# Layer 1 of a two-layer convolution and recurrence kernel: half of each normalized column copied across the partitions by GpSimd instead of by DMA transfers

## The chip, the cores and the metric

The kernel runs on one core of a Trainium2 chip. Its time is the device time of one execution in microseconds (us). The core has five engines that matter here: TensorE for matrix products (in the profile PE, with PEld for the loading of its weights), VectorE (DVE), ScalarE (ACT), GpSimd (POOL) and SyncE (SP), which in this kernel only issues transfers. Each engine has its own stream of instructions and works through it in order. Transfers (DMA) run beside the engines, on 16 DMA engines that all queues share. An engine waits for another, or for a transfer, by a semaphore.

## The reference

An image batch x of shape 4 x 64 x 256 x 256 (images, channels, rows, columns) goes through two layers, each x + f(groupnorm(x)). Layer 0 is a 1x1 and a 3x3 convolution, a product of spectra over 8x8 patches, a norm over channels and a gate. Layer 1, which the change touches, is a recurrence over the columns of the image:

```python
x = x + _L0_conv_ref(_gn(x), ...)
x = x + _L1_conv_ref(_gn(x), ...)
# inside _L1_conv_ref, f[w] is column w of the normalized image, (images, rows, channels)
def step(prev_col, cur_col):
    nb = jnp.concatenate([pad, prev_col, pad], axis=1)
    x = jnp.concatenate([nb[:, :-2], nb[:, 1:-1], nb[:, 2:]], axis=-1)
    new = _gru_cell(x, cur_col, w_ih, w_hh, b_ih, b_hh)   # shapes left out
    return (new, new)
_, outs = jax.lax.scan(step, f[0], f[1:])
```

The cell takes three rows of the previous column's result as input (192 channels in, "taps") and the current column as its hidden value ("own", 64 channels in). It has three gates: r and z by a sigmoid, n by a tanh, and new = (1 - z) n + z h. Column w can't be finished before column w - 1 is: 255 steps, each over 4 images x 256 rows x 64 channels.

## The kernel before

Layer 0 works in 32 blocks and takes about the first 4299 us; the change leaves it as it is. Between the layers stand a few small operations for the second group norm.

Layer 1 keeps a column of the four images as a tile of 128 partitions by 2 slots by 256 rows. A partition half holds the 64 channels of one image, so that four images fill two halves times two slots. Which image lies where changes from column to column: SLOTS lists slot by slot the images of the two halves, ((0, 1), (2, 3)) for even columns and ((0, 2), (1, 3)) for odd ones. The reason is the matrix unit. One matmul here uses a quarter of it, 64 rows by 64 columns, and quarters() issues four that can run side by side, one for each pair (r, c) of an input half r and an output half c. The taps read the previous state at half r, slot c and write the result at half c, slot r. So a column comes out with halves and slots exchanged, and the odd and even layouts follow from that.

The own part of a column must land in the same place, at half c, slot r. For r = c the normalized column xn has it in the right half. For r and c different, the image lies in the wrong partition half: its input must first be brought to the other half. That is what the tile xt is for: it holds, for each of 8 columns of a block, the two images that must cross over, slot 0 of the second half in the first half, and slot 1 of the first half in the second half. In column(), own() reads xn for r == c and xt otherwise.

The stages of a column and who does them:

- load_columns(w) issues, on SP's queue, three transfers for two columns of raw values, 16 columns ahead of their use. raws has three buffers of 8 columns (WB = 8).
- normalize(w, slot) is one ScalarE activation per slot. It is called for column w + 8 inside state(w, part), after the r gate's sigmoid of that part: slot 0 in part 0, slot 1 in part 1. So the normalized columns, and xt, run 8 columns ahead of their use. xns and xts have two buffers of 8 columns.
- In normalize, after slot 1 of every odd column, two transfers on SP's queue fill xt for two columns.
- column(w) issues the matmuls. A column is worked in two parts of its rows. parts(w) sets the cut, which moves up by one row per column and jumps back every 32 columns (SKEW), so that a part needs only rows of the previous column that are already done; part 0 has from 144 down to 113 rows. For each part: own and taps of r, for part 0 also own of n for the whole column, then taps of n, own and taps of z.
- state(w, part) turns the sums into the new state: sigmoid r (ACT), n = (hn + b) r + in (two VectorE operations that read the sums), sigmoid z and tanh (ACT), then g = (z - 1) h, n z, and st = n z - g on VectorE.
- add(w), on GpSimd, adds the state to the raw column, 128 x 512; after each odd column three transfers on SP's queue write the pair of columns out.
- empty_states(n) zeroes, on GpSimd, the edge rows of the next block of states, once every 8 columns.

The program order of the engines is the order in which the code issues. Ahead of the loop stand the loads of 16 columns, the normalizing of columns 0 to 8 with their xt, and empty_states(0). In the loop over w come empty_states for the next block (every 8 columns), column(w) with its two states (and in them normalize of column w + 8), add(w), and after odd columns load_columns. On SP's queue a pair of columns is therefore two xt transfers, three of out, three of raw, each waiting in its turn; on GpSimd's there is one add per column and two memsets per 8 columns.

All of the kernel's instructions pass through a helper that keeps the program order (line 158), so the profile names line 158 for nearly all of them; rows are told apart by their tiles: pshr, pshn, psni, pshz are the sums of the gates, st the state, wh and wi the weights of own and taps.

Of the kernel before, what the change touches and what calls it, by code (L numbers as in the profile page):

```python
# [16 lines left out]
B, C, W, H = 4, 64, 256, 256  # L17
# [146 lines left out]
def tile_conv_then_gru(  # L164
# [18 lines left out]
    nc = InOrder(tc, tc.nc)  # L183
# [109 lines left out]
    with layer0 as s:  # L293
# [20 lines left out]
        def normalize(n, jq):  # L314

            t, b, at = xq[n, jq], n // 8, n % 8
            flat = t.rearrange("p j k -> p (j k)")
            shift, rstd = sc0[:, b, 0:1], sc0[:, b, 1:2]
            if jq == 3:
                nc.vector.tensor_scalar(flat, flat, rstd, shift, ALU.mult, ALU.add)  # L320
            else:
                nc.scalar.activation(flat, flat, AF.Identity, bias=shift, scale=rstd)
            grid = t.rearrange("p j (r c) -> p j r c", c=10)
            if jq % 2 == 0:
                nc.gpsimd.memset(grid[:, 0, :, 0:1], 0.0)
            else:
                nc.gpsimd.memset(grid[:, 15, :, 9:10], 0.0)
            if at == 0 and jq < 2:
                nc.gpsimd.memset(grid[0:C, :, 0, :], 0.0)
            if at == 7 and jq >= 2:  # L330
                nc.gpsimd.memset(grid[C:P, :, 9, :], 0.0)
# [297 lines left out]
        for jq in range(4):  # L629
            normalize(0, jq)  # L630
        norm = None
        for n in range(NBLK + 1):
# [60 lines left out]
            for k in range(8):  # L693
                if k in (0, 3, 6):
                    pv = psum(4)
                    values(n, k, pv[:, 0:2])
                elif k in (1, 4, 7):
                    values(n, k, pv[:, 2:4])
                    keep_values(k - 1, 2, pv)
                else:  # L700
                    pv = psum()
                    values(n, k, pv)
                    keep_values(k, 1, pv)
                if k in (0, 2):
                    next(norm)
                if k in (1, 2, 4) and n + 1 < NBLK:
                    normalize(n + 1, k // 2)
                if k in (3, 4, 6):
                    next(norm)
                if k == 5 and n + 1 < NBLK:  # L710
                    normalize(n + 1, 3)
# [24 lines left out]
    with ExitStack() as s:  # L736
# [4 lines left out]
        raws, xns, xts, stcols = {}, {}, {}, {}  # L741
# [15 lines left out]
        def new_columns(n):  # L757
            xns[n] = colp.tile([P, 2, WB, H], F32, tag="xn", name=f"xn_{n}")
            xts[n] = colp.tile([P, WB, H], F32, tag="xt", name=f"xt_{n}")
# [6 lines left out]
        def normalize(w, slot):  # L766
            n, i = w // WB, w % WB
            if i == slot == 0:
                new_columns(n)
            nc.scalar.activation(  # L770
                xns[n][:, slot, i],
                raws[n][:, slot, i],
                AF.Identity,
                bias=sc1[:, w % 2, slot, 0:1],
                scale=sc1[:, w % 2, slot, 1:2],
            )
            if slot and i % 2:

                for half in range(2):
                    nc.sync.dma_start(  # L780
                        xts[n][half * C : (half + 1) * C, i - 1 : i + 1],
                        xns[n][(1 - half) * C : (2 - half) * C, half, i - 1 : i + 1],
                    )

        def add(w):
# [96 lines left out]
        for w in range(W):  # L882
            n, i = w // WB, w % WB
# [68 lines left out]
```

## Time and profile before

| | us |
|---|---|
| median of 3 runs | 5828.33 |
| lowest and highest run | 5819.98, 5828.91 |
| the profiled execution's own time | 5838.45 |
| its span, first to last instruction | 5836.7 |

The profile shows one execution. Busy time is the time in which an engine worked on an instruction; it does not tell whether anybody waited for it. Times on the timelines are counted from the start of the span. In a row, "out<-in" are the program's tiles, the shape is partitions x elements, "x" a count; in brackets stands how long the engine had been idle before, and what ended that. "issue" as the releaser means that nothing the profile shows had been waited for. A row of a queue (SPq) is the issuing of a transfer, not the transfer itself.

GpSimd's share of layer 1 before (from 4300 us on, columns: operation, tiles, shape and count, then busy us, mean ns of one, and idle time before with its releasers):

```profile
L158 POOL TENSOR_TENSOR raw<-raw,st 128x512 f32<-128x512 f32 x256 | 303.4, 1185 | 1151.4 <-ACT xn L158 569.2 <-DVE st L158 353.4 <-DMA raw<-x 156.6
L158 POOL MEMSET st<- 128x16 f32 x60 | 5.1, 128 | 71.2 <-PE pshz L158 71.2
```

Of the page's list of transfers these belong to layer 1 (count and size of each):

```profile
raw<-x SPq DMA_DIRECT2D x128, 256.0 KB
raw<-x SPq DMA_DIRECT2D x256, 128.0 KB
xt<-xn SPq DMA_DIRECT2D x256, 128.0 KB
out<-raw SPq DMA_DIRECT2D x128, 256.0 KB
```

The list is cut there at its end; the smaller transfers of out are not on the page.

### The profile page before, as it was taken

How to read it: one execution, taken by the hardware profiler on the slowest of the kernel's cores; microseconds unless marked ns; L12 is line 12 of the kernel's file. 1: busy time of each engine (PE TensorE's matmuls, PEld its weight loads, DVE VectorE, ACT ScalarE, POOL GpSimd, SP SyncE). 2: the span in 40 equal slices, each digit the busy share in tenths (PEclk: the TensorE clock that was granted, in tenths of full speed). 3: DMA queues.
4: the chain of work that ended last, by engine and by line, in shares of the span. 5: the costliest groups of instructions: out<-in, count | busy, mean ns of one | idle time of the engine just before them, and what ended most of it. 6: DMA issues, size and time to landing. Idle time of an engine off the chain costs nothing. (4 is left out here: it accounts for less than half of the span.)

```text
span 5836.7 us, 278467 instructions
## 1 busy us (share of the span) xinstructions
PE 5472.7 (94%) x127204; PEld 4752.8 (81%) x127204; DVE 4076.5 (70%) x9593; ACT 3475.0 (60%) x4604; POOL 476.3 (8%) x749
## 2 busy tenths in 40 slices
PE   4999999999999999999999999999979999999998
PEld 3888888778878888888878888888768888888888
DVE  4777677777777777766777677666667776777766
ACT  3656666556566666556556666565556665666655
POOL 0000000000000000000000000000002221222212
PEclk9999999999999999999999999999989999999999
DMA  7555555555555555555555554544444444444443
GB/s 251 149 153 157 154 155 142 149 158 150 152 150 156 154 146 141 160 149 148 151 144 152 143 134 130 145 133 129 136 116 115 117 114 112 115 117 116 119 112 84
DMA packets 557274, 818.28 MB, mean 140 GB/s; under 512 B 37484, under 2 KB 431632, under 8 KB 553712
## 3 DMA queue, kind: packets, MB, share of 16 engines
q1 hardware_dynamic: 522256, 634.46, 40.4%
q0 software_dynamic: 33552, 165.43, 8.9%
q8 instruction: 996, 16.32, 1.2%
q14 instruction: 182, 1.49, 0.1%
q10 hardware_dynamic: 288, 0.58, 0.0%
HBM read 622.72 MB, written 144.05 MB: 131 GB/s over the span
## 5 line engine op out<-in xcount | busy, mean ns | idle before, releaser
L158 PEld LDWEIGHTS psring<-h,t 100*32 100x32 f32 x40960 | 1333.4, 115 | 303.9 <-issue 200.6
L158 PE MATMUL psring<-h,t 100*32 100x128 f32 x40960 | 1445.3, 274 | 115.3 <-issue 41.4
L158 PEld LDWEIGHTS psring<-w_sb,xq 64*100 64x100 f32 x24576 | 1355.8, 163 | 81.4 <-issue 51.1
L158 PE MATMUL psring<-w_sb,xq 64*100 64x128 f32 x24576 | 1399.9, 271 | 21.6 <-issue 7.6
L158 ACT COPY h<-psring 100x1024 f32<-100x1024 f32 x1274 | 1205.7, 1026 | 162.8 <-PE psring L158 154.4
L158 DVE TENSOR_TENSOR pr<-psring,q 128x512 f32<-128x512 f32 (+1 forms) x576 | 462.9, 857 | 336.5 <-PE psring L158 326.4
L158 DVE BATCH_NORM_STATS2 lnst<-z 128x6 f32<-128x64 f32 x4096 | 545.7, 216 | 117.6 <-ACT z L158 117.6
L158 DVE TENSOR_TENSOR z<-z,lnm 128x1024 f32<-128x1024 f32 x512 | 612.8, 1218 | 8.7
L158 ACT COPY q<-psring 128x1024 f32<-128x1024 f32 x256 | 259.3, 1013 | 527.4 <-PE psring L158 445.3
L158 ACT ACTIVATE z<-pshz,b_rz 128x288 f32<-128x288 f32 (+7 forms) x510 | 242.5, 476 | 520.6 <-PE pshz L158 520.6
L158 PE MATMUL pshr<-st,wi 64*64 64x144 f32 (+7 forms) x12240 | 511.2, 270 | 42.0 <-issue 26.1
L158 ACT COPY z<-psring 128x2048 f32<-128x2048 f32 x128 | 238.9, 1867 | 520.9 <-PE psring L158 520.9
L158 PE MATMUL pshz<-st,wi 64*64 64x144 f32 (+7 forms) x12240 | 513.0, 271 | 25.3 <-issue 24.0
L158 PE MATMUL psni<-st,wi 64*64 64x144 f32 (+7 forms) x12240 | 510.2, 270 | 21.0 <-issue 20.0
L158 PE MATMUL psring<-pr,g_sb 32*64 32x512 f32 x8192 | 488.7, 599 | 5.2 <-issue 5.1
L158 ACT ACTIVATE y<-psring,ln_sb 128x512 f32<-128x512 f32 x512 | 372.1, 780 | 201.5 <-PE psring L158 199.0
L158 PEld LDWEIGHTS psni<-st,wi 64*64 64x64 f32 x12240 | 447.1, 133 | 41.9 <-issue 30.1
L158 PEld LDWEIGHTS pshr<-st,wi 64*64 64x64 f32 x12240 | 422.2, 133 | 57.5 <-issue 54.8
L158 PEld LDWEIGHTS pshz<-st,wi 64*64 64x64 f32 x12240 | 427.0, 133 | 38.4 <-issue 37.7
L158 DVE COPY h<-psring 100x1024 f32<-100x1024 f32 x262 | 320.1, 1222 | 171.8 <-PE psring L158 167.9
L158 DVE SCALAR_TENSOR_TENSOR g<-z,xn 128x288 f32<-128x288 f32 (+7 forms) x510 | 218.4, 428 | 311.9 <-ACT z L158 310.3
L158 DVE TENSOR_TENSOR y<-psring,y 128x1024 f32<-128x1024 f32 x256 | 312.4, 1221 | 128.8 <-ACT y L158 127.9
(100 smaller groups left out, 7342.4 us busy)
## 6 DMA issues: line engine op xcount, KB each, us to landing
t<-t_all SPq DMA_DIRECT2D x768, 400.0 KB
xq<-in_xh POOLq DMA_DIRECT2D x128, 800.0 KB, 4.6
xr<-in_x SPq DMA_DIRECT2D x256, 256.0 KB
x<-xr SPq DMA_DIRECT2D x256, 256.0 KB
raw<-x SPq DMA_DIRECT2D x128, 256.0 KB
raw<-x SPq DMA_DIRECT2D x256, 128.0 KB
xt<-xn SPq DMA_DIRECT2D x256, 128.0 KB
out<-raw SPq DMA_DIRECT2D x128, 256.0 KB
```

Source lines behind the costliest of these rows:

```text
L158: return self.tc.keep_in_program_order(got(*args, **kwargs))
```

## The change

In normalize, the two transfers that fill xt after every odd column are replaced by two GpSimd copies after every column. They move the same values: for each half of the partitions, one image of 64 channels by 256 rows from the other half. The transfers moved two columns at a time, the copies move one.

```diff
-            if slot and i % 2:
+            if slot:
 
                 for half in range(2):
-                    nc.sync.dma_start(
-                        xts[n][half * C : (half + 1) * C, i - 1 : i + 1],
-                        xns[n][(1 - half) * C : (2 - half) * C, half, i - 1 : i + 1],
+                    nc.gpsimd.tensor_copy(
+                        xts[n][half * C : (half + 1) * C, i], xns[n][(1 - half) * C : (2 - half) * C, half, i]
                     )
```

256 transfers leave SP's queue, and 512 copies of 64 x 256 join GpSimd's: in the loop two ahead of each add, and 18 in the prologue, where they stand ahead of the memsets of empty_states(0). TensorE's first matmul of a column that reads xt waited for the transfers, once per two columns, and now waits for GpSimd, once per column. The matmuls and the work of ScalarE and VectorE are the same, in the same order.

## The prediction

> **What bounds the kernel now.** I read first the page (engines, slices), then the busy time by stretches of layer 1, then the waits of layer 1, then the timeline at two places: the start of layer 1 and a stretch in its middle. Last I went through the trace's own records of DMA packets and weight loads, because the waits left a question open. The change touches layer 1 alone, which begins at about 4303 us with the loads of raw and ends with the span.
>
> ```profile
> PE 5472.7 (94%) x127204; PEld 4752.8 (81%) x127204; DVE 4076.5 (70%) x9593; ACT 3475.0 (60%) x4604; POOL 476.3 (8%) x749
> ...
> 4740.00:5140.00 400.00, 369.73 (x12280) 352.46 (x12284) 277.15 (x668) 239.50 (x534) 79.74 (x84) 0.99 0.42 113
> 5140.00:5540.00 400.00, 374.67 (x12632) 356.73 (x12628) 284.84 (x686) 245.80 (x548) 83.20 (x85) 1.00 0.43 117
> ...
> PEld pshr L158 <- issue: 67.7, 95, 2.2
> ...
> PEld pshz L158 <- issue: 46.6, 76, 1.5
> PE pshr L158 <- issue: 31.1, 51, 1.5
> ```
>
> The second and third lines give, for 400 us each, the busy time of PE, PEld, DVE, ACT and POOL, then clock, DMA share and GB/s. PE is busy 92 to 94%, VectorE 70%, GpSimd 20%, and DMA 42% without being anybody's named releaser. So TensorE bounds layer 1, and what it loses is put down to "issue": no semaphore explains it. Its loads wait for no data there. The timeline of weight loads shows when:
>
> ```profile
> 5000.55 0.31 PEld L158 LDWEIGHTS psni<-st,wi 64*64 64x64 f32 x11 [0.60 <-issue]
> 5004.57 0.30 PEld L158 LDWEIGHTS pshz<-st,wi 64*64 64x64 f32 x11 [0.35 <-issue]
> 5012.06 0.13 PEld L158 LDWEIGHTS pshz<-xt,wh 64*64 64x64 f32 x2 [0.28 <-issue]
> 5016.08 0.13 PEld L158 LDWEIGHTS pshr<-xt,wh 64*64 64x64 f32 x2 [0.38 <-issue]
> ```
>
> The stalls come 4.0 us apart (5000.55, 5004.57; 5012.06, 5016.08) and at different matmuls each time. The DMA queues of 4340 to 5730 us have something with that period:
>
> ```profile
> q1 hardware_dynamic: 150869, 154.57, 40.7%
> q8 instruction: 339, 5.55, 1.7%
> ...
> xt<-xn SPq DMA_DIRECT2D x236, 128.0 KB
> ```
>
> Queue 8 fetches instructions: 339 packets in 1390 us, each of 16384 bytes by the packet records, one per 4.1 us. In those records 237 of 340 fetches are followed by a hole of over 0.2 us in the weight loads that ends 1.24 to 1.57 us (5th to 95th hundredth) after the packet's end; so TensorE waits for instructions. Matmul starts over 0.25 us apart, from 4340 us on, are 220 with 162 us in sum. A fit over pairs of columns gives column time = 5.26 us + 0.99 x (such gaps in it), correlation 0.93; the mean is 5.885 us, (5829.12 - 4334.27)/254 by the ends of the state writes. Some 0.65 us of every column is thus waiting for instructions, and it is paid in full.
>
> **What the Trainium skill says.** "Runtime: NRT & Kernel Launch", Instruction fetch mechanics: an engine's instructions come in 16 KiB blocks of 256 over a DMA queue that the sequencer drives, and the cost is "mostly hidden". The trace has the 16384-byte packets; it does not agree that they are hidden here (162 us). "DMA: Bandwidth & Descriptors", Issuing engines are not separate DMA queues: all transfers share 16 DMA engines whoever issued them; the trace agrees in so far as fetches start later under traffic (below). "SBUF — State Buffer", Who interferes with whom: a VectorE instruction with two SBUF inputs contends with a GpSimd instruction that reads SBUF, and the later one blocks. No row of before settles this. "GPSIMD Engine Reference", Engine selection: a one-input operation runs at roughly line rate; no GpSimd copy stands in this trace.
>
> **The change part by part.**
>
> *Start of layer 1.* Here the xt transfers are on the path.
>
> ```profile
> 4309.02 0.74 PE L158 MATMUL pshr<-xn,wh 64*64 64x144 f32 x2 [6.86 <-ACT xn L158]
> 4323.07 1.31 PE L158 MATMUL pshr<-xt,wh 64*64 64x144 f32 x3 [13.31 <-DMA xt<-xn]
> ...
> 4303.73 15.06 SPq L158 DMA_DIRECT2D raw<-x  x24
> 4318.89 13.48 SPq L158 DMA_DIRECT2D xt<-xn  x10
> ...
> 4308.37 8.39 ACT L158 ACTIVATE xn<-raw,sc 128x256 f32<-128x256 f32 x16 [0.27 <-DMA raw<-x]
> 4316.78 1.28 ACT L158 ACT_TABLE_LOAD   x1
> ```
>
> TensorE stands 13.31 us for the first xt, which SP can issue only after 24 loads (15.06 us). Changed, the copies of column 1 can be done by about 4310.5. But the zeroing of the state's edges (empty_states) now stands behind all 18 prologue copies on GpSimd, and the first taps need it. The last normalize ends at 4308.37 + 8.39 = 4316.76; one more copy and the memsets (0.13 us each) bring the taps to about 4317.5, against 4324.00 now. Gain 6.5 us. The sigmoid table is loaded by 4318.06, before the first taps end, so it hides. If a copy takes over 0.5 us, GpSimd falls behind ScalarE's 0.52 us per normalize and 2 us of it is lost; fetches during the raw loads (DMA share 0.98 there) can take another 1 to 2. I take 6, bounds 3 and 7.
>
> *Instruction fetch.* Removed are 256 transfers of 128 KB, 236 of them in the 1390 us. By the packet records xt is 15104 packets of 2048 bytes and 2067 us of DMA engine time there, raw and out 6846 us: xt is 22% of it, 8.9% of the 16 engines. What a fetch pays for it: after a stall ended, the next fetch began 1.19 us later in the mean where neither raw/out (under 10% load) nor xt moved in the first 1.2 us (69 cases), 1.41 where xt moved alone (42), 2.04 where raw/out were over 60% and xt still (64). xt was there in 80 of 236, so 0.34 x 0.22 = 0.075 us per fetch, plus 0.26 us per unit load in the fetch's own length (fit) x 0.089 = 0.023. Over the 363 fetches from 4340 us on: 36 us, of which the 70% that stall anyway pass it on: 25. A direct fit of stall on load gives 0.83 x 0.089 x 363 = 27; a fit of the start delay on both loads gives only 0.26 x 0.113 + 0.023 = 0.052, so 13. I take 20, bounds 5 (other traffic fills the place) and 36 (stall falls with engine time, 22% of 162).
>
> *The copies on GpSimd.* 512 of 64x256. Bounds: a 64x160 memset, which reads nothing, takes 0.227 us, so 0.3 at least; the add, 1.185 us for 512 elements from two inputs, is 2.1 ns per element beyond a memset's 0.11, so 0.64 at most. I take 0.42. Two per column are 0.84 us; with the add 2.03 of 5.9 us: GpSimd does not become the bound, and the copies serve a column 8 later (47 us), which hides their length. Behind them on the queue is add(w), which waits for the end of the column's state in any case: laid over this trace, no add would start later, even with copies of 1.0 us.
>
> *The port.* Laid over this trace (each copy at the end of its normalize or of the add ahead), 40 to 50% of copies of 0.30 to 0.45 us overlap one of the two-input VectorE operations g, n x z, st (0.43 us each), 33 to 57 us in all. If VectorE loses half, that is 16 to 28 us over 510 halves of columns, some 0.05 us each, against a slack between state write and its first tap of 0.63 us in the median (first part) and 0.86 (second). Only 33 of 254 columns, at the start of the 32-column skew, have under 0.08. I take +3, bounds 0 and 8.
>
> *Waits and SP.* TensorE's two waits for transfers per column pair become two for GpSimd per column; both were met 8 columns earlier: 0. SP loses 0.51 us per issue and two waits; the first out of a pair goes some 2.5 us earlier, raw and the other outs still wait for the second add: 0. The last 8 columns have no copies either way.
>
> Sum: -6 - 20 + 3 = -23 us. The profiled execution's own time is 5838.45 (span 5836.7), 10 us over the median of 5828.33. 5838.45 - 23 = 5815.5, a ratio of 0.9961; on the median that is 5805.
>
> **The rivals.**
> *Only the start (20%).* Fetches are late because of raw and out, which come in bursts; for: 2.04 against 1.41 us. Against: xt alone adds 0.22. Then -6, and 5822.
> *Stalls fall with the load, or more (15%).* All latencies lie near the time of a page, so that little makes a stall. 22% of 162 = 36, with the start 42: 5786.
> *The port (10%), slower.* A copy across partitions takes 1 us or more, holds VectorE in g, n x z or st of both parts, and the state comes after TensorE needs it. It decides from 23/254 = 0.09 us per column beyond the slack. With 1.0 us copies the overlap on this trace is 176 us; at 0.2 us per column beyond the slack, 51 us, net +28: 5856. Against: nothing near has that length. (Only from (5.885 - 1.185)/2 = 2.35 us per copy would GpSimd itself be the bound.)
> That the copies don't replace the transfers is ruled out by the code: the same halves of xt are written from the same halves of xn, one column at a time.
>
> **How the numbers follow.** A change of 0.2% (11.7 us) is what a measurement here can tell from none. The likeliest, 55%, is 5805, with an own range of 5790 to 5818 from its bounds. Faster by over 0.2% (under 5816.7): the likeliest but for its upper edge, 52%, and 15%: 67%. Within: 20 and 3: 23%. Slower: 10%. The range of 5779 to 5832 holds all but the port's rival and the fringe of the stronger gain.
>
> **What would show it.** In the changed profile: the idle before the first taps of column 1 shrinks by 6 us, with taps near 4317.5; copies of 0.3 to 0.64 us; the DMA share of layer 1 falls from 0.42 to about 0.33; "issue" before PEld falls by about an eighth and column time from 5.885 to about 5.82; the VectorE rows of g, n and st stay near 0.43 us. Wrong would be: the same issue time with the xt packets gone (then only the start stays), or VectorE rows above 0.5 us with TensorE waiting for st.

## The result, and the profile after

| | us |
|---|---|
| changed, median of 4 runs | 5786.96 (5771.76 to 5788.57) |
| before, median of 4 runs | 5824.15 (5813.40 to 5828.91) |
| ratio | 0.9933, 95% interval 0.991 to 0.9956 |
| profiled execution of the changed kernel | 5771.76 (span 5770.0) |

The changed kernel is faster by 0.67%, 37 us. Its profiled execution was the fastest of its runs, and that of before (5838.45 us) was slower than all its other runs: the spans differ by 66.7 us, and not all of that is the change. I cut both spans at the same marks. From the start to the beginning of the second small matmul of the norm between the layers (gn_pv), a stretch in which the kernels are the same, 4301.6 us became 4292.7: 8.9 us that are not the change. From there to the first taps of column 1, 22.4 became 15.8. From the end of column 1 to the end of column 255, 1494.8 became 1445.1. The rest is 1.5 us.

The start of layer 1 after, on the timelines of TensorE and GpSimd:

```profile
4299.90 0.74 PE L158 MATMUL pshr<-xn,wh 64*64 64x144 f32 x2 [6.61 <-ACT xn L158]
4300.58 0.95 PE L158 MATMUL pshr<-xt,wh 64*64 64x144 f32 x3
...
4308.49 1.72 PE L158 MATMUL pshr<-st,wi 64*64 64x144 f32 x24 [6.71 <-POOL st L158]
...
4306.37 1.88 POOL L158 COPY xt<-xn 64x256 f32<-64x256 f32 x4 [0.21 <-ACT xn L158]
4308.31 0.26 POOL L158 MEMSET st<- 128x16 f32 x4
```

The wait of 13.31 us for the transfer is gone, the matmuls with xt follow at once. The taps then stand 6.71 us for the memset of the state's edges, which runs behind the last of the 18 copies: the wait that took the place of the old one.

The loop after, by the same stretches as before (busy us of PE, PEld, DVE, ACT, POOL, then clock, DMA share, GB/s), the waits of TensorE in it (what was waited for, us in total, times, longest), and its DMA queues from 4340 to 5660 us:

```profile
4740.00:5140.00 400.00, 380.32 (x12811) 363.30 (x12804) 292.52 (x697) 249.13 (x558) 142.57 (x228) 0.99 0.34 96
5140.00:5540.00 400.00, 383.42 (x13016) 367.41 (x13011) 296.31 (x707) 252.86 (x566) 144.30 (x227) 1.00 0.34 96
...
PEld pshz L158 <- issue: 36.5, 62, 1.4
PEld pshr L158 <- issue: 21.3, 52, 1.7
...
PEld pshr L158 <- DVE st L158: 15.9, 7, 2.3
PE pshr L158 <- DVE st L158: 14.0, 7, 2.1
...
q1 hardware_dynamic: 129914, 121.67, 32.0%
q8 instruction: 332, 5.44, 1.7%
```

PE is busy 95 to 96% in place of 92 to 94%. The idle time put down to "issue" looks halved (pshr and pshz together 58 us, against 114), but a part of it only changed its label. Every 32 columns, where the cut between the parts jumps back, a weight load waits some 2.2 us for the state, in both kernels. After, these seven waits are the row of 15.9 us; before, they stand under "issue" (2.1 to 2.2 us each). And 7.4 us that the changed profile puts down to GpSimd's xt end 1.3 to 1.6 us after a fetch's packet, as the stalls do; the copy waited for was made 8 columns earlier. Like with like it is 81 us against 114, 29% less.

The DMA share fell from 0.42 to 0.34; the 2048-byte packets are gone, and the loop fetches as many instruction packets as before (364). By the trace's records the gaps of over 0.25 us between matmul starts sum to 103 us after and 162 before, in 151 and 220 gaps. Those that end 1.2 to 1.7 us after a fetch's packet make up 146 us before (212 gaps) and 84 us after (136); the seven waits for the state are 15 and 16 us of the rest. A column takes 5.69 us in place of 5.885.

GpSimd and VectorE in layer 1 after (mean ns of one stands behind the busy time; both rows are of the changed kernel's later profile on a third chip, called after_p below):

```profile
L158 POOL COPY xt<-xn 64x256 f32<-64x256 f32 x462 | 193.2, 418 | 276.8 <-ACT xn L158 245.7 <-DVE st L158 8.4 <-DMA out<-raw 5.7
...
L158 DVE TENSOR_TENSOR n<-n,z 128x280 f32<-128x280 f32 (+7 forms) x462 | 205.6, 445 | 13.6 <-ACT n L158 11.0
```

A copy takes 0.418 us, from 0.392 to 0.714 by its single records. The two-input VectorE operation n x z went from 0.426 us (shown below, before_p) to 0.445 us.

### The profile page after: what moved, and what is told of

It is laid out like the page before. It is cut to its first block, busy times and chain, and to the rows that moved or that the text cites. A ratio compares the mean times of both kernels' runs of the same rounds, so it can differ in the third digit from the quotient of the medians.

```text
span 5770.0 us, 278646 instructions
## 1 busy us (share of the span) xinstructions
PE 5459.7 (95%) x127204; PEld 4740.7 (82%) x127204; DVE 4085.6 (71%) x9593; ACT 3474.0 (60%) x4604; POOL 690.3 (12%) x1261
## 4 chain that ended last, share of the span: by engine, by line
PE 68%; issue 3%; ACT 2%; DMA 2%; DVE 1%; SPq 0%; POOL 0%; POOLq 0%; ACTq 0%; DVEq 0%
PE psring L158 44%; PE pshz L158 8%; PE pshr L158 8%; PE psni L158 6%; DMA t<-t_all 2%; PE pshn L158 2%; ACT v L158 1%; ACT z L158 1%; ACT h L158 0%; DVE z L158 0%; DVE lnst L158 0%; DVE pr L158 0%; SPq L158 0%; ACT xq L158 0%; POOL raw L158 0%
## 5 line engine op out<-in xcount | busy, mean ns | idle before, releaser
L158 PE MATMUL pshr<-st,wi 64*64 64x144 f32 (+7 forms) x12240 | 527.2, 271 | 28.8 <-DVE st L158 14.0
L158 PE MATMUL pshz<-st,wi 64*64 64x144 f32 (+7 forms) x12240 | 528.6, 270 | 14.3 <-issue 13.0
L158 PE MATMUL psni<-st,wi 64*64 64x144 f32 (+7 forms) x12240 | 529.3, 271 | 10.3 <-issue 9.6
L158 PEld LDWEIGHTS pshr<-st,wi 64*64 64x64 f32 x12240 | 438.8, 133 | 41.7 <-issue 17.5
L158 PEld LDWEIGHTS pshz<-st,wi 64*64 64x64 f32 x12240 | 443.6, 133 | 24.5 <-issue 23.4
```

What stands on the lines that cost most here:

```text
L158: return self.tc.keep_in_program_order(got(*args, **kwargs))
```

## The experiments

Kernels sent together ran on one chip, beside runs of the kernel before. The chips differ: the median of before was 5812.8, 5878.5 and 5818.1 us for the three sets. So I compare ratios, and spans or loops only within a set. "Loop" is from the end of column 1 to the end of column 255, "gaps" are those of over 0.25 us between matmul starts in it, both from the trace's records.

### Which part of the change counts

after_again is the changed kernel unaltered. e1 and e2 do the change in the prologue alone, or in the loop alone:

```diff
 # e1_start (e2_loop: the two conditions exchanged, w > WB + 1)
-            if slot:
+            if slot and w <= WB + 1:
                 for half in range(2):
                     nc.gpsimd.tensor_copy(
...
+            elif slot and i % 2:
+                for half in range(2):
+                    nc.sync.dma_start(
...
```

> The changed kernel once more, on the same chip as the next three, as the mark they are held against. Both theories: about 0.993 of the kernel before. The profile of before was the slowest of its runs and that of after the fastest, so I expect the time per column of layer 1 here between 5.69 and 5.77 us, not again a loop shorter by 50 us.

> GpSimd copies only for columns 0 to 9, transfers as before for all later ones. Theory (instruction fetches are late behind the xt transfers): only the gain of the start is left, first taps some 6.6 us earlier, so 0.9989 of the kernel before, and 5.85 to 5.9 us per column. Rival (the start is what counts, traffic does nothing): the same as the changed kernel, 0.993.

> Transfers for columns 0 to 9, GpSimd copies for all later ones. Theory: the start is as before (first taps 22 us after the norm's last matmul), the loop as in the changed kernel, together 30 us less, 0.995. Rival (only the start): no change, 1.000.

| | ratio to before (95%) | gn_pv to first taps | loop | gaps |
|---|---|---|---|---|
| after_again | 0.9903 (0.9885 to 0.9922) | 16.2 | 1446.6 | 108 |
| e1_start | 0.9992 (0.9978 to 1.0005) | 16.3 | 1487.3 | 153 |
| e2_loop | 0.9928 (0.9911 to 0.9946) | 21.8 | 1441.3 | 108 |

The same stretch of e1 and of e2:

```profile
5140.00:5540.00 400.00, 374.02 (x12575) 356.35 (x12571) 282.86 (x682) 244.65 (x547) 82.27 (x87) 1.00 0.42 117
...
5140.00:5540.00 400.00, 380.21 (x12906) 367.45 (x12901) 294.00 (x702) 250.57 (x562) 141.73 (x228) 1.00 0.34 97
```

The start gains its 6 us where it was changed and nowhere else; as a ratio this can't be told from none. The loop is what counts: 1441 and 1447 us with copies, 1487 with transfers. So e2 came out under the 0.995 that I had expected, and its interval leaves that out. I had expected the loop of after_again to be longer than in the first profile; it was the same (1446.6 against 1445.1). Its ratio is lower than that of the first runs, 0.9933; the two intervals overlap.

### Is it the traffic, or the wait for it

```diff
 # e3_traffic: the changed kernel, and
+            if slot and i % 2 and w > WB + 1:
+                for half in range(2):
+                    nc.sync.dma_start(
+                        xds[n][half * C : (half + 1) * C, i - 1 : i + 1],
+                        xns[n][(1 - half) * C : (2 - half) * C, half, i - 1 : i + 1],
+                    )
```

Nobody reads xds.

> The changed kernel, and from column 10 on the two transfers per pair of columns are still made, of the same values into a tile that nobody reads. Theory (the traffic delays the fetches): the loop goes back to before or slightly over it, 5.85 to 5.9 us per column and 0.999; the DMA share of layer 1 is 0.42 to 0.43 again. Rival (what cost time was TensorE's wait for the transfers, or what stood behind it): nobody waits for these transfers, so it stays at 0.993.

The ratio was 0.9991 (0.998 to 1.0003), the loop 1485.0 us, the gaps 149. The two stretches of its loop, and its queues and the unread transfers from 4740 to 5540 us:

```profile
4740.00:5140.00 400.00, 372.59 (x12535) 352.41 (x12531) 285.93 (x682) 243.74 (x547) 137.83 (x220) 1.00 0.42 116
5140.00:5540.00 400.00, 377.08 (x12640) 356.68 (x12632) 288.83 (x689) 245.85 (x550) 139.20 (x224) 1.00 0.43 117
...
q1 hardware_dynamic: 87626, 89.71, 40.6%
...
xd<-xn SPq DMA_DIRECT2D x137, 128.0 KB
```

Here TensorE waits for no transfer, GpSimd copies as in the changed kernel (POOL 138 us), and nobody reads what is moved. With the DMA share back at 0.42 the whole gain of the loop is gone. So the gain is not from a wait that went, and the copies do not carry the loss: the transfers' presence does. The records also show where the time goes. After a stall has ended, the next fetch begins 1.54 to 1.57 us later in the mean where the transfers run (before, before_p, e1, e3), and 1.32 to 1.39 us later where they don't (after, after_again, after_p, e2). The fetch's packet itself takes the same in both, 1.08 to 1.11 us. So the fetch begins later; it does not last longer.

What e3 leaves open is which side of the presence does it. On SP's queue the first out of each pair stands behind the transfers of xt in e3 as it did before, so e3 brings back both their bytes and that delay.

### How much traffic costs how much

```diff
 # e5_half: from column 10 on, the first half of xt by GpSimd, the second by a transfer
-                for half in range(2):
+                for half in range(2 if w <= WB + 1 else 1):
...
+            if slot and i % 2 and w > WB + 1:
+                nc.sync.dma_start(xts[n][C:P, i - 1 : i + 1], xns[n][0:C, 1, i - 1 : i + 1])
 # e4_double: the kernel before, and each pair of transfers a second time into xds
```

> The kernel before, and from column 10 on each pair of transfers into xt is made a second time into a tile that nobody reads: twice the xt traffic. The traffic cost 45 us of the loop from none to once (1445 us in the changed kernel, 1485 to 1495 where it flows). Theory A, stall in proportion to the traffic: another 45, loop 1535 us, 1.008. Theory B, many fetches lie just under the time of a page, so that the first traffic costs most and more of it less: 10 to 25 us, 1.002 to 1.004. Theory C, each fetch behind it gets later still and nearly all now stall: 60 or more, over 1.010.

> The changed kernel, but from column 10 on the second partition half of xt is filled by a transfer per pair of columns again and the first by GpSimd: half the xt traffic, half the copies. Theory A (proportion): loop 1445 + 22 = 1467 us, 0.994. Theory B (the first traffic costs most): 1475 or more, 0.996.

Half the traffic gave 0.9949 (0.9931 to 0.9968), near the middle between none (0.990) and once (1). That lies between theory A's 0.994 and theory B's 0.996, and its interval holds both. Twice gave 1.0004 (0.999 to 1.0017): the second helping is almost free, cheaper than the 1.002 to 1.004 of theory B. The loops of this chip (1511 us for half, 1544 for twice) can't be held against the 1445 of the expectations, since it was slower in every kernel. The second set had no profile of the kernel before, so I took one, with the changed kernel and the doubled one beside it on a third chip:

> The kernel before, for a profile from the same chip as the next three; the chip of the last four was slower in every kernel, so loops of different chips are not held against each other. Loop 1485 to 1540 us, gaps in the matmuls 150 to 205 us.

> The changed kernel, for the same. Loop 40 to 60 us under that of the kernel before beside it, gaps 45 to 60 us fewer.

> Twice the xt traffic, once more, for its profile beside one of the kernel before. Theory B, as the last run of it left it (the second traffic costs at most a fifth of the first): loop 0 to 12 us over the kernel before. Theory A (proportion): 45 us over it.

| xt traffic | loop | gaps | 2048-byte packets, share of 16 engines | raw and out |
|---|---|---|---|---|
| none (after_p) | 1446.0 | 104 | 0 | 0.310 |
| once (before_p) | 1492.2 | 159 | 0.091 | 0.301 |
| twice (e4d_double) | 1501.1 | 167 | 0.181 | 0.302 |

From none to once 46 us, from once to twice 9, which is no more than loops with the transfers once differ by among themselves (1485 to 1495 us). For the step from once to twice theory A is out, and what is left is theory B's direction with less than it said; where between none and once the bend lies, the half dose doesn't tell. One stretch of each of the three, in the order of the table:

```profile
5140.00:5540.00 400.00, 380.79 (x12968) 364.49 (x12964) 295.70 (x705) 251.34 (x564) 144.42 (x228) 1.00 0.34 97
```

```profile
5140.00:5540.00 400.00, 369.29 (x12412) 352.53 (x12412) 280.26 (x674) 241.18 (x539) 81.81 (x84) 1.00 0.42 115
```

```profile
5140.00:5540.00 400.00, 368.80 (x12277) 350.56 (x12280) 277.80 (x667) 238.98 (x532) 80.39 (x83) 0.99 0.51 135
```

The DMA share rises 0.34, 0.42, 0.51; PE's busy time falls by 11.5 us, then by 0.5.

Where in the cycle of two columns the gaps lie says more. I summed them by their distance from the end of the odd column's add, after which SP issues two of out and three of raw. By where they start, the cycle of before_p has 1.30 us of gaps, that of after_p 0.87 (the cycle is 11.8 and 11.4 us long). In the three microseconds from -1 to +2 they fell from 0.34 to 0.04, and from +4 to +8 (around the turn of the cycle) from 0.72 to 0.58. In before_p the traffic of xt and the first out fills -6 to -1; in after_p that out moved up to about -6 to -3, and from -3 to +1 nothing moves. SP's timelines of before_p and after_p show the move:

```profile
5012.96 4.27 SPq L158 DMA_DIRECT2D xt<-xn  x2
5017.32 4.67 SPq L158 DMA_DIRECT2D out<-raw  x3
5022.04 1.90 SPq L158 DMA_DIRECT2D raw<-x  x3
```

```profile
5012.42 1.84 SPq L158 DMA_DIRECT2D raw<-x  x3
5016.12 8.48 SPq L158 DMA_DIRECT2D out<-raw  x3
5024.65 1.91 SPq L158 DMA_DIRECT2D raw<-x  x3
```

The three outs now begin some 8.5 us ahead of the next raw in place of 4.7: the first follows its own add. So a part of the gain could be that stretch without traffic, about as long as the 4 us between two instruction fetches, and not the bytes as such. e5_half, which keeps the out behind a transfer and halves the bytes, still gave half the gain, so the bytes or the packets' number have a part. e7 below bears on the rest.

### The copies themselves

```diff
 # e6_nocopy
-            if slot:
+            if slot and w <= WB + 1:
 # and in new_columns, for blocks after the first
+                nc.gpsimd.memset(xts[n], 0.0)
```

> The changed kernel with copies for columns 0 to 9 only: from column 10 on nothing is brought across, xt is zeroed once per block by GpSimd, so the crossing half of the own part is left out of the result (TensorE still does its matmuls). What is gone is the copies alone. Prediction's step (the shared port costs 3 us, hidden in the slack of the state): loop within 3 us of 1445, VectorE's g and n x z back from 0.44 to 0.43 us. Rival (the port costs more, since columns whose first part waits for the state rose from 33 to 59): 10 us or more under 1445.

The ratio was 0.9897 (0.9861 to 0.9932), against 0.9903 for the changed kernel on another chip. The loop of 1473 us can't be held against 1445, for the reason given above; that expectation was badly put. VectorE in before_p, and without copies in e6:

```profile
L158 DVE TENSOR_TENSOR n<-n,z 128x280 f32<-128x280 f32 (+7 forms) x448 | 190.9, 426 | 10.2 <-ACT n L158 8.5
...
L158 DVE TENSOR_TENSOR n<-n,z 128x226 f32<-128x226 f32 (+7 forms) x454 | 193.5, 426 | 12.5 <-ACT n L158 10.8
```

n x z is back at 0.426 us from 0.445, so GpSimd's copies do slow two-input VectorE operations. TensorE's wait for the state did not grow with it (13.4 us by the profile of before_p and 14.0 of after_p, for PE pshr), and the time shows no cost that this comparison could see; its interval is some 20 us to either side, so a few us would not show.

### Two tries at a better version

e7_split sends raw and out in equal portions after each column; e8_edges moves empty_states(0) ahead of the prologue's copies.

```diff
 # e7_split, in the loop over w
             if i % 2 and w + 2 * WB < W:
-                load_columns(w + 2 * WB - 1)
+                load_columns(w + 2 * WB - 1, (0,))
+            if i % 2 == 0 and w and w + 2 * WB - 1 < W:
+                load_columns(w + 2 * WB - 2, (1, 2))
 # and in add: the first out after even columns, the other two after odd ones
 # e8_edges
+        empty_states(0)
         for w in range(WB + 1):
             for slot in range(2):
                 normalize(w, slot)
-        empty_states(0)
```

> The changed kernel, its raw and out transfers dealt out evenly: after even columns one of out and the two small ones of raw, after odd columns the two small ones of out and the large one of raw, 512 KB each, in place of 256 and 768 KB. Theory (a fetch is late by what lies ahead of it, so long bursts cost most): gaps in the matmuls fall from 105 to 80 us or less, loop 1420. Rival (what counts is the share of the time with traffic, which stays at 31%): loop within 8 us of 1445, 0.990 to 0.993.

> The changed kernel with the zeroing of the first state's edges moved ahead of the 18 copies on GpSimd. If the taps of column 1 wait for nothing else, they start some 7 us earlier, but the sigmoid behind them still waits for ScalarE's 18 normalizes and its table load: 3 us less than the changed kernel, 0.9900. Rival (the half clock of TensorE after its idle time eats it): no gain at all, the end of column 1 as far from the norm as in the changed kernel, 25 us.

e7 gave 0.9913 (0.9885 to 0.9941), with gaps of 144 us against 137 in e6 on the same chip. Shorter bursts brought no fewer gaps; the theory behind e7 falls, and its ratio is the one that the rival named.

e7 also bears on the stretch without traffic. The longest one in a cycle is 4.8 us in the mean in after_p and in e6, 2.4 in before_p, and 2.9 in e7, which moves the same bytes as the changed kernel. The gaps from -1 to +2 came back in e7 (0.28 us per cycle, against 0.06 in e6), but the cycle as a whole has 1.20 us of them against 1.14. So most of the gain does not need that stretch: the gaps that it empties come up elsewhere. That leaves, as the main part, the bytes, the packets' number or SP's issuing of them. These were not separated, and no run moved the first out alone, with the transfers in place.

e8 gave 0.9896 (0.9879 to 0.9912), not to be told from the changed kernel. Its first taps start 8.2 us after gn_pv, not 16, but column 1 ends 24.2 us after it, against 24.7 in the first profile of the changed kernel and 26.2 in after_p, on e8's chip. The wait moved on, to the sigmoid behind ScalarE's prologue:

```profile
4299.68 1.09 ACT L158 ACTIVATE xn<-raw,sc 128x256 f32<-128x256 f32 x2 [0.87 <-DMA raw<-x]
4300.79 1.28 ACT L158 ACT_TABLE_LOAD   x1
4302.08 0.50 ACT L158 ACTIVATE g<-pshr,b_rz 128x288 f32<-128x288 f32 x1
```

The rival, TensorE's clock, did not decide it: the granted clock is 0.50 from 4291 to 4294 us, but the sums of r are done by 4294.6, and the sigmoid that reads them starts at 4302.08.

## Why the prediction was right, and which term was too small

**What bounds the loop.** Right: instruction fetches that come late, with transfers as their cause. e3 settles it that the transfers' presence costs the time and no engine's wait for them does. I read it a little too wide: of the 162 us of gaps 15 are the seven waits for the state, so fetches cost 0.58 us of a column and not 0.65. And over the 1390 us that I named, 2067 us of xt are 9.3% of the 16 engines, not 8.9%, which moves no term by more than 2 us.

**The start.** I wrote -6 with taps at about 4317.5. By the marks it was 22.4 - 15.8 = 6.6 us (taps 15.8 us after gn_pv; on the marks of before that is 4317.4). The 18 copies kept pace with ScalarE, and the memset behind them was the new wait.

**The fetch term.** This is the term that was mis-sized: -20, with bounds 5 and 36. The loops say -46 (third chip) and -50 (first profiles), port included. The first runs' 37 us less the start's 6.6 leave 30. Both readings lie above 20, and the loops lie above my upper bound, which came from the share of engine time (22% of 162); the gaps fell by a third (159 to 104). I had priced xt by fits within one profile: what a fetch pays if xt moves while it waits. By the gaps that follow a fetch, the mean stall per fetch is 0.40 us before and 0.23 after (146 and 84 us over 364 fetches), a fall of 0.17, of which xt's own coefficient explains 0.07 (0.83 x 0.089). The rest the fit had charged to raw and out or to no load at all; that a fit within one run can't see what the transfers do to the rest of the traffic is my reading of it, not shown.

**"The first out of a pair goes some 2.5 us earlier: 0".** The move is there, but the zero was asserted, not worked out. The place where the gaps vanished, at the end of the stretch that it left empty, spoke for a share in the gain; e7 speaks against a large one.

**The copies.** I took 0.42 us, measured 0.418. GpSimd did not become the bound (36% busy), and the adds did not hold anything up.

**The port.** +3 with bounds 0 and 8. VectorE's g and n x z grew by 12 and 19 ns, 16 us over the layer, the lower end of the 16 to 28 that I wrote. Of columns whose first part starts its taps as soon as the state is there, 33 became 59 of 254, but TensorE's waits for it summed to the same 14 us, and e6, which has no copies, has 51: most of that rise comes with the faster TensorE. What the Trainium skill says in "SBUF — State Buffer", Who interferes with whom, that a VectorE instruction with two SBUF inputs contends with a GpSimd instruction that reads SBUF, is borne out in kind by e6 (0.426 us without copies, 0.445 with them). That the slack hides it agrees with the runs, within intervals too wide to confirm 3 us.

**The rivals.** "Only the start" falls with e1 (0.9992, and a loop of 1487 us). "The port" as a loss falls with the ratio. "Stalls fall with the load, or more" named 5786, and was nearer to the result than my likeliest case, whose own range, 5790 to 5818, begins 3 us above the result (the bounds of its terms, added up, would have given 5785 to 5828). The fall was more than in proportion to the load taken away, though e4 shows that the load added on top costs almost nothing. That the result stands within 1 us of this rival's number is luck: its 36 us for the fetches is under the 46 to 50 of the loops, and the median of before was 4 us lower in the result than the one that I started from. Of what would show it, column time (5.69, not 5.82) and "issue" (29% less like with like, not an eighth) went further than I wrote; the DMA share (0.34, not 0.33) and the copies as written.

## What to carry to other kernels

When TensorE bounds a stretch and its idle time is put down to "issue" at a regular distance in time, look at the instruction queue's packets: in e3, transfers that nobody waits for cost the whole gain of the loop there. Before comparing the "issue" rows of two profiles, see whether the same wait stands under another name in one of them. Handing a transfer within the core to an idle engine can then be worth more than the transfer's own wait. Price it by taking it out, not by a fit within one profile, and look at what moves up on the queue that it leaves.

## What the hardware showed that I had not expected

The stall is not in proportion to the traffic: on one chip, gaps of 104, 159 and 167 us for none, one and two portions of xt, the second portion adding 9 us of loop, which is within what such loops differ by, to the first's 46. And a chip can differ by more than the change is worth: the same kernel before had medians of 5812.8, 5878.5 and 5818.1 us on the three, with the TensorE clock at 0.992 to 0.995 in all profiles of them.
